# Cross-attention outputs as latents by features, with a column of ones in the values

## Chip, cores and metric

The kernel runs on one core of a Trainium2 chip. The metric is the device time of one execution in microseconds. It is float32 throughout, except where the reference rounds to fp8, which the kernel does by arithmetic on VectorE. In the profile PE is TensorE, PEld its weight loads, DVE VectorE, ACT ScalarE, POOL GpSimd and SP the engine that issues most transfers.

## What is computed

One block of a perceiver: 128 latents of 512 features attend to 12,544 context tokens, then to each other, then pass through a mixture of 32 experts. Nearly all the work is the cross-attention to the context, which, cut to what matters, is

```
k = ctx @ w_k ; v = ctx @ w_v              # 12544 x 1024 each: 8 groups of 128
k = layernorm(k) per group
for g in 8 groups, for the 2 query heads of g:
    p   = softmax(q_h @ k_g.T / sqrt(128))  # 128 latents x 12544 tokens
    out = p @ v_g                           # 128 latents x 128 features
x += fp8_linear(concat(out) / smooth)       # rounded to fp8, then projected to 512
```

## The kernel before

**Chunks.** The tokens go through in 25 chunks `c`, 24 of 512 tokens and one of 256 in the middle (`c = 12`). The softmax is a running one: after each chunk the maxima may grow, and what has been summed so far (`ol[g]`) is scaled down by `exp(old - new)`.

**One chunk.** First the keys of chunk `c` are made (`keys`, `k_chunk`), then for `g` = 0 to 7 `scores(c, g)` alternates with a step of the values (`v_chunk`); the outputs of chunk `c` (`outputs(c, g)`) are spread over the making of the keys of chunk `c + 1`. In `scores`, PE multiplies the keys (tokens stationary) by the queries of two heads, 256 columns, so that a tile `s` has 128 token rows (partitions) and 4 x 256 columns: four token blocks by 2 heads x 128 latents. ACT evicts it from PSUM with the key's norm as a scale (line 919, below called S0 to S7 by group).

**Maxima, shift and exponential.** `maxima` calls `max_rows` for groups in fours; it makes `sh`, the number to subtract, and `als`, the old maxima less the new. `spread(c, j)` then treats groups `2j` and `2j + 1`: DVE spreads `sh` over all partitions by a transposition into PSUM (`b_ps`, line 974), does the same for the scale factors (`al`, in SBUF), and subtracts the shift from both groups' `s` (line 992, one instruction of 128 x 1024 for each group). `weigh` takes the exponential on ACT (line 1004, below E0 to E7 by group), scales `ol[g]` on POOL (line 1006), and adds on POOL the four blocks of `s` into the second half of `ol[g]` (line 1014): sums by lane, which become the softmax's denominators at the very end.

**Outputs.** `outputs` has the values stationary and the 256 columns of `s` moving, four accumulating matmuls for each group; each float32 matmul shows in the profile as two passes, each with its own weight load. The result is 128 features x 256, and DVE adds it to `ol[g]` (line 1027).

**The values.** `v_chunk` makes the values by a Strassen scheme: PSUM banks are accumulated into in several products, and between two products ACT copies the state of a bank out. In

```
            mm(a, 5, False)
            u2 = kept(a, "u2")
            mm(d, 2, False)
            nc.vector.tensor_tensor(t2[:, :H], d, u2, ALU.add)
            mm(a, 6, False)
```

`kept` is an ACT copy of bank `a` (line 439). Product 6 adds to that bank, so PE can't begin it before ACT has made the copy; product 2, into another bank, lies between them. In the profile these are line 562: product 5 is `a_ps<-wsum,mix`, product 2 is `c_ps<-wsum,ctx`, product 6 is the second `a_ps<-wkv,ctx`.

**Order.** Engines work through their own queues in order and wait for each other by semaphores. A scheduler decides at build time, by its own estimate of durations, in which order each queue holds its instructions; `tc.issue_after` only adds a bound. So the program has a fixed order on each engine, which can be read from the built program.

**The end.** After the last chunk `lane_sums` sums the lanes by matmuls with a column of ones, `finished` turns the reciprocals into columns of all partitions and scales, `round_block` rounds to fp8, and `proj` projects, four blocks. Some `spin` matmuls lie between. Then follow self-attention and the experts.

Of the kernel before, what the change touches and what calls it, by code (L numbers as in the profile page):

```python
# [45 lines left out]
def block_kernel(  # L46
# [223 lines left out]
    V = vp.tile([P, CH // P, G * D], F32, name="V")  # L270
# [103 lines left out]

    def v_unit(c, v):

        nt = chunks[c][1] // P

        def mm(ps, i, first):
            w, x = mixed_w[i], mixed[c][i]  # L380
            for k in range(2):
                last_mm[0] = nc.tensor.matmul(
                    ps, lhsT=x[:, k, v * P : (v + 1) * P], rhs=w[:, k, H : 2 * H],
                    start=first and k == 0, stop=k == 1, skip_group_check=True,
                ).ins

        t1, t2 = V[:, v, :], V[:, nt // 2 + v, :]
        return unit(mm, lambda t: t, t1[:, :H], t2[:, :H], t1[:, H:], t2[:, H:])
# [132 lines left out]
    def v_chunk(c):  # L521
# [10 lines left out]
        def both(t):  # L532
            return t.rearrange("p (i o) -> p i o", i=2)

        def to(o, v):
            return V[:, v, :].rearrange("p (i c o) -> p i c o", i=2, c=2)[:, :, o, :]

# [20 lines left out]
        for v in range(2):  # L558
            def mm(ps, i, first):
                w, x = mixed_w[i], mixed[c][i]  # L560
                for k in range(2):
                    last_mm[0] = nc.tensor.matmul(  # L562
                        ps, lhsT=x[:, k, v * P : (v + 1) * P], rhs=w[:, k, H : 2 * H],
                        start=first and k == 0, stop=k == 1, skip_group_check=True,
                    ).ins

            t1, t2 = V[:, v, :], V[:, 2 + v, :]
            a, d = bank("a_ps"), bank("c_ps")
            mm(a, 0, True)
            nc.vector.tensor_tensor(t1[:, :H], a, t1[:, :H], ALU.add)  # L570
            mm(d, 4, True)
            nc.scalar.copy(t2[:, H:], d)
            yield
            mm(a, 5, False)
            u2 = kept(a, "u2")
            mm(d, 2, False)
            nc.vector.tensor_tensor(t2[:, :H], d, u2, ALU.add)
            mm(a, 6, False)
            nc.vector.tensor_tensor(t2[:, H:], a, t2[:, H:], ALU.add)
            added[0] = nc.vector.tensor_tensor(t1[:, H:], a, t1[:, H:], ALU.add).ins  # L580
            yield
# [63 lines left out]
    with tc.tile_pool(name="pre", bufs=2) as pre, tc.tile_pool(name="pre1", bufs=1) as pre1, tc.tile_pool(  # L645
# [248 lines left out]
    ol = [olp.tile([P, 2, HS], F32, name=f"ol{g}") for g in range(G)]  # L894
    rlat = keep.tile([S, NH], F32, name="rlat")
# [3 lines left out]
        tc.tile_pool(name="ps_so", bufs=3, space=PSUM, side="right", reuse_waits="tile")  # L899
    )  # L900
    ps_t = late.enter_context(
        tc.tile_pool(name="ps_t", bufs=2, space=PSUM, side="right", reuse_waits="tile")
    )
    prob, mxr, mrun, shifts, rescale, lsum, summed = {}, {}, {}, {}, {}, {}, [None]
# [28 lines left out]
    def max_rows(c, j0, n):  # L933
# [29 lines left out]
        if c:  # L963
            al = small.tile([P, 32], F32, tag="als", name="als", bufs=3)[:, : 16 * n]
            nc.vector.tensor_tensor(al, old[:, : 16 * n], m, ALU.subtract)  # L965
            nc.scalar.activation(al, al, AF.Exp, scale=scale)  # L966
        for j in range(j0, j0 + n):
            x = slice(16 * (j - j0), 16 * (j - j0) + 16)
            mrun[j] = m[:, 16 * (j - j0) :]
            shifts[j] = sh[:, x], al[:, x] if c else None  # L970

    def to_all(dst, src):

        nc.vector.transpose(  # L974
            dst.rearrange("p h (k i) -> p (h k) i", i=32),
            src[:, :, None].to_broadcast([P, 16, 32]),
        )

    def spread(c, j):

        nt = chunks[c][1] // P
        sh, al = shifts.pop(j)
        ps = ps_t.tile([P, 2, HS], F32, tag="t", name="b_ps")

        with tc.issue_after(added[0]) if whole(c) and j == 2 else nullcontext():
            to_all(ps, sh)
        if c:
            rescale[j] = tmp.tile([P, 2, HS], F32, tag="al", name="al")
            to_all(rescale[j], al)
        for a in range(2):  # L990
            s = prob[2 * j + a]
            nc.vector.tensor_tensor(  # L992
                s[:, :nt, :], s[:, :nt, :], ps[:, a, None, :].to_broadcast([P, nt, HS]),
                ALU.subtract,
            )

    def weigh(c, j, after=None):

        nt = chunks[c][1] // P
        for a in range(2):  # L1000
# [4 lines left out]
            if c:  # L1005
                nc.gpsimd.tensor_tensor(  # L1006
                    ol[g], ol[g], rescale[j][:, a, None, :].to_broadcast([P, 2, HS]), ALU.mult
                )
                first = ol[g][:, 1, :]
            else:  # L1010
                first = s[:, 0, :]

            for t in range(0 if c else 1, 2 if c == NCH - 1 and g >= G - 2 else nt):
                summed[0] = nc.gpsimd.tensor_tensor(ol[g][:, 1, :], first, s[:, t, :], ALU.add).ins  # L1014
                first = ol[g][:, 1, :]

    def outputs(c, g):
        nt = chunks[c][1] // P
        s = prob.pop(g)
        ps = ps_so.tile([D, HS], F32, tag="s", name="o_ps")  # L1020
        for t in range(nt):
            end = nc.tensor.matmul(  # L1022
                ps, lhsT=V[:, t, g * D : (g + 1) * D], rhs=s[:, t, :],
                start=t == 0, stop=t == nt - 1,
            )
        if c:
            nc.vector.tensor_tensor(ol[g][:, 0, :], ol[g][:, 0, :], ps, ALU.add)  # L1027
        else:
            nc.vector.tensor_copy(ol[g][:, 0, :], ps)
        return end.ins  # L1030

    def lane_sums(g, last):

        if g % 4 == 0:
            lsum[g // 4] = ps_t.tile([S, 8], F32, tag="t", name="l_ps")
        ps = lsum[g // 4]
        for h in range(2):
            i = g % 4 * 2 + h
            x = slice(h * S, (h + 1) * S)
            terms = [ol[g][:, 1, x]] + [t[:, x] for t in last]  # L1040
            for t, y in enumerate(terms):
                end = nc.tensor.matmul(
                    ps[:, i : i + 1], lhsT=y, rhs=ones[:, 0:1], start=t == 0,
                    stop=t == len(terms) - 1,
                )
        if g % 2:
            nc.vector.reciprocal(rlat[:, 2 * g - 2 : 2 * g + 2], ps[:, g % 4 * 2 - 2 : g % 4 * 2 + 2])
        return end.ins

    def finished(b):  # L1050


        ps = ps_so.tile([P, 4, S], F32, tag="s", name="ps_inv")
        r0 = _COLS["smooth"][0] + 16 + 4 * b
        for h in range(4):
            end = nc.tensor.transpose(
                ps[:, h, :], rlat[:, 4 * b + h : 4 * b + h + 1].to_broadcast([S, P]), ident
            )
        for h in range(4):
            o = ol[2 * b + h // 2][:, 0, (h % 2) * S : (h % 2 + 1) * S]  # L1060
            nc.vector.scalar_tensor_tensor(
                o, o, rcol[:, r0 + h : r0 + h + 1], ps[:, h, :], ALU.mult, ALU.mult
            )
# [20 lines left out]
    for c in range(NCH):  # L1084
# [7 lines left out]
        for g in range(G):  # L1092
# [10 lines left out]
            if g == 2 and c + 1 < NCH:  # L1103
                with tc.issue_after(summed[0] if c else made):
# [25 lines left out]
    with ExitStack() as rest:  # L1130
# [18 lines left out]
        def round_block(b):  # L1149
            cq = post.tile([P, 4, S], F32, tag="cq", name="cq")  # L1150
            rounded(post, cq, [ol[2 * b + a][:, 0, :].rearrange("p (h s) -> p h s", h=2) for a in range(2)])
            return cq
# [11 lines left out]
        last = {g: prob[g] for g in (G - 2, G - 1)}  # L1164

        def sums_of(g):
            return lane_sums(
                g, [last[g][:, t, :] for t in range(2, CH // P)] if g in last else []
            )

        spare = pps.tile([P, H], F32, tag="ps", name="spare")

# [8 lines left out]

        cqs = {}
        maxima(c, 8)
        outputs(c, 0)
        maxima(c, 9)
        outputs(c, 1)
        outputs(c, 2)
        maxima(c, 10)
        end = outputs(c, 3)
        with tc.issue_after(end):  # L1190
            sums_of(0)
            sums_of(1)
        outputs(c, 4)
        end = outputs(c, 5)
        with tc.issue_after(end):
            finished(0)
            cqs[0] = round_block(0)
            sums_of(2)
            end = sums_of(3)
        with tc.issue_after(end):  # L1200
            outputs(c, 6)
            end = outputs(c, 7)
        with tc.issue_after(end):
            finished(1)
            cqs[1] = round_block(1)
            sums_of(4)
            end = spin(spare[:, :240], sums_of(5), 4)
        with tc.issue_after(end):
            end = proj(0, cqs[0]).ins
        with tc.issue_after(end):  # L1210
            finished(2)
            cqs[2] = round_block(2)
            sums_of(6)
            end = spin(spare[:, :240], sums_of(7), 1)
        with tc.issue_after(end):
            end = finished(3)
            cqs[3] = round_block(3)
        for b in (1, 2, 3):
            with tc.issue_after(end):
                end = proj(b, cqs[b]).ins  # L1220


        mask = post1.tile([P, 4, P], F32, name="mask")
        with tc.issue_after(summed[0]):
# [27 lines left out]
        with tc.tile_pool(name="po_s", bufs=1, space=PSUM, reuse_waits="tile") as pss:  # L1252
# [68 lines left out]
            with tc.issue_after(summed[0]):  # L1321
# [190 lines left out]
```

## Time and profile before

| | |
|---|---|
| median of 3 runs (lowest, highest) | 2119.5 us (2119.05, 2121.09) |
| span of the profiled execution | 2117.6 us |
| PE busy | 2092.5 us, 99% of the span |
| PEld, weight loads, beside PE | 1584.7 us, 75% |
| DVE busy | 1508.2 us, 71% |
| POOL busy | 1180.5 us, 56% |
| ACT busy | 907.8 us, 43% |
| mean granted TensorE clock | 0.997 |

The profile has no other time of the profiled execution than its span, from its first to its last instruction; the median of the runs is 1.9 us more. Matmuls are pipelined and the ends that the profile gives for them are modelled, so how fast they go is best read from the distance between their starts. Busy time of an engine other than PE says how much room it has, not what it costs.

### The profile page before, as it was taken

To read this page: it belongs to the slowest core of one execution; us is meant where nothing else is said; L and a number is where in the kernel's file an instruction comes from. 1 tells how busy PE (TensorE), PEld (TensorE's weight loads), DVE (VectorE), ACT (ScalarE), POOL (GpSimd) and SP (SyncE) were. 2 spreads that over 40 slices of the span, in tenths; PEclk is the share of its full clock that TensorE was granted. 3 is DMA by queue.
4 is the path that set the end of the run, shared out by engine and by line. 5 is a ranking of instruction groups with operands and counts; after the bars stand their busy time and mean duration, and the time that the engine had idled before them with its cause. 6 is when DMAs were issued, how large, how long until landed. Compare 5 with 4: busy or idle time off the path is not lost.

```text
span 2117.6 us, 25404 instructions
## 1 busy us (share of the span) xinstructions
PE 2092.5 (99%) x9087; PEld 1584.7 (75%) x9087; DVE 1508.2 (71%) x2875; ACT 907.8 (43%) x1687; POOL 1180.5 (56%) x1359
## 2 busy tenths in 40 slices
PE   8999999999999999999999999999999999999999
PEld 3667877877887787787777877787787778776554
DVE  8787777678678767866878678767867876786211
ACT  3445455445435544543444445444544544441111
POOL 5345675575576557558675576567557656743000
PEclk9999999999999999999999999999999999999999
DMA  9300000000000000000000000000000000008693
GB/s 324 119 21 1 21 21 0 21 20 21 1 21 21 0 21 20 11 1 21 21 21 20 1 21 20 1 21 20 16 6 21 21 1 21 1 6 303 189 286 108
DMA packets 71231, 95.59 MB, mean 45 GB/s; under 512 B 3136, under 2 KB 39488, under 8 KB 71104
## 3 DMA queue, kind: packets, MB, share of 16 engines
q1 hardware_dynamic: 70816, 93.92, 13.4%
q8 instruction: 71, 1.16, 0.2%
q14 instruction: 56, 0.46, 0.1%
q10 hardware_dynamic: 288, 0.04, 0.0%
HBM read 93.69 MB, written 0.26 MB: 44 GB/s over the span
## 4 chain that ended last, share of the span: by engine, by line
PE 92%; DVE 3%; issue 2%; POOL 1%; ACT 1%; DMA 0%; SPq 0%; POOLq 0%; DVEq 0%; ACTq 0%
PE s_ps L914 15%; PE o_ps L1022 15%; PE a_ps L458 11%; PE a_ps L562 11%; PE c_ps L458 7%; PE c_ps L562 7%; PE gu_ps L1427 4%; PE fa_ps L527 4%; PE fa_ps L449 4%; PE moe_acc L1448 2%; PE fc_ps L449 2%; PE fc_ps L527 2%; PE ps_p L710 2%; PE fb_ps L527 1%; PE fb_ps L449 1%
## 5 line engine op out<-in xcount | busy, mean ns | idle before, releaser
L1014 POOL TENSOR_TENSOR ol<-ol,s 128x256 f32<-128x256 f32 x764 | 549.9, 731 | 46.6 <-ACT s L1004 9.9
L1022 PE MATMUL o_ps<-s,V 128*128 128x256 f32 x1568 | 371.5, 379 | 0.9 <-DVE ol L1027 0.9
L914 PE MATMUL s_ps<-qxT,KT 128*128 128x256 f32 x1568 | 370.2, 379 | 0.4 <-ACT s L919 0.4
L919 ACT ACTIVATE s<-s_ps,krs 128x256 f32<-128x256 f32 x784 | 320.9, 472 | 107.8 <-PE s_ps L914 77.2
L1006 POOL TENSOR_TENSOR ol<-ol,al 128x512 f32<-128x512 f32 x192 | 243.5, 1280 | 209.6 <-DVE al L974 209.6
L914 PEld LDWEIGHTS s_ps<-qxT,KT 128*128 128x128 f32 x1568 | 297.8, 190 | 74.1 <-issue 36.4
L619 POOL TENSOR_TENSOR krs<-kve,mhalf 128x16 f32<-128x16 f32 (+1 forms) x50 | 142.9, 2858 | 358.9 <-DVE kve L617 358.9
L925 DVE TRANSPOSE_TENSOR_REDUCE mxr<-s 128x32 f32<-128x1024 f32 (+1 forms) x200 | 243.9, 1220 | 117.2 <-ACT s L919 115.6
L1022 PEld LDWEIGHTS o_ps<-s,V 128*128 128x128 f32 x1568 | 291.4, 190 | 37.9 <-ACT s L1004 1.3
L1004 ACT ACTIVATE s<-s 128x1024 f32<-128x1024 f32 (+1 forms) x200 | 203.6, 1040 | 85.1 <-DVE s L992 84.7
L992 DVE TENSOR_TENSOR s<-s,b_ps 128x1024 f32<-128x1024 f32 (+1 forms) x200 | 231.5, 1177 | 0.0
L591 ACT ACTIVATE sq<-KT 128x1024 f32<-128x1024 f32 (+1 forms) x100 | 103.8, 1040 | 228.2 <-DVE KT L477 220.8
L1027 DVE TENSOR_TENSOR ol<-ol,o_ps 128x256 f32<-128x256 f32 x192 | 77.7, 405 | 157.3 <-PE o_ps L1022 152.4
L562 PE MATMUL a_ps<-wkv,ctx 128*128 128x512 f32 x368 | 172.9, 592 | 0.0
L458 PE MATMUL a_ps<-ctx,wkv 128*128 128x256 f32 x736 | 170.3, 379 | 0.0
L458 PEld LDWEIGHTS a_ps<-ctx,wkv 128*128 128x128 f32 x736 | 138.1, 190 | 18.1 <-ACT u L439 0.3
L595 DVE TRANSPOSE_TENSOR_REDUCE sqr<-sq 128x32 f32<-128x1024 f32 (+1 forms) x104 | 121.0, 1168 | 4.9 <-ACT sq L591 4.9
L477 DVE TENSOR_TENSOR KT<-a_ps,KT 128x512 f32<-128x512 f32 x138 | 90.0, 681 | 44.1 <-PE a_ps L458 43.4
L562 PEld LDWEIGHTS a_ps<-wkv,ctx 128*128 128x128 f32 x368 | 69.9, 190 | 68.4 <-issue 66.0
L439 ACT COPY u<-fa_ps 128x512 f32<-128x512 f32 x92 | 54.0, 587 | 102.3 <-PE fa_ps L449 100.0
L966 ACT ACTIVATE als<-als 128x32 f32<-128x32 f32 x48 | 11.0, 229 | 198.1 <-DVE als L965 198.1
L1427 PE MATMUL gu_ps<-gu,xT 128*128 128x384 f32 x256 | 87.4, 486 | 0.0
(314 smaller groups left out, 3321.6 us busy)
## 6 DMA issues: line engine op xcount, KB each, us to landing
ctx<-in_ctxT SPq DMA_DIRECT2D x23, 1024.0 KB, 5.0
gu<-in_w SPq DMA_DIRECT2D x32, 384.0 KB, 5.0
gu<-in_v SPq DMA_DIRECT2D x32, 384.0 KB, 5.7
dn<-in_w SPq DMA_DIRECT2D x16, 768.0 KB, 5.5
w<-in_wprojT SPq DMA_DIRECT2D x8, 1024.0 KB, 5.7
w<-in_wqxT SPq DMA_DIRECT2D x4, 1024.0 KB, 11.2
w<-in_wqT SPq DMA_DIRECT2D x4, 1024.0 KB, 5.1
wkv<-in_wkvT SPq DMA_DIRECT2D x8, 256.0 KB, 8.2
```

What stands on the lines that cost most here:

```text
L449: nc.tensor.matmul(ps[:, j * P : (j + 1) * P], lhsT=f[n][:, i, g * D : (g + 1) * D], rhs=xs[i][n], start=first and j == 0, stop=True, skip ...
L458: nc.tensor.matmul(ps[:, j * h : (j + 1) * h], lhsT=w[:, k, (2 * u + j) * D : (2 * u + j + 1) * D], rhs=x[:, k, :], start=first and j == k ...
L562: last_mm[0] = nc.tensor.matmul(ps, lhsT=x[:, k, v * P : (v + 1) * P], rhs=w[:, k, H : 2 * H], start=first and k == 0, stop=k == 1, skip_g ...
L914: end = nc.tensor.matmul(ps[:, t - t0, :], lhsT=KT[:, g, t * P : (t + 1) * P], rhs=qxT[:, 2 * g : 2 * g + 2, :], start=True, stop=True,)
L919: copied[0] = nc.scalar.activation(s[:, t, :], ps[:, t - t0, :], AF.Copy, scale=rs[:, t : t + 1]).ins
L925: nc.vector.tensor_reduce(mxr[g // 4][:, g % 4, :nt, :].rearrange("p t k -> p (t k)"), s[:, :nt, :].rearrange("p t (k i) -> p (t k) i", i=32),
L992: nc.vector.tensor_tensor(s[:, :nt, :], s[:, :nt, :], ps[:, a, None, :].to_broadcast([P, nt, HS]), ALU.subtract,)
L1004: nc.scalar.activation(s[:, :nt, :], s[:, :nt, :], AF.Exp, scale=scale)
L1006: nc.gpsimd.tensor_tensor(ol[g], ol[g], rescale[j][:, a, None, :].to_broadcast([P, 2, HS]), ALU.mult)
L1014: summed[0] = nc.gpsimd.tensor_tensor(ol[g][:, 1, :], first, s[:, t, :], ALU.add).ins
L1022: end = nc.tensor.matmul(ps, lhsT=V[:, t, g * D : (g + 1) * D], rhs=s[:, t, :], start=t == 0, stop=t == nt - 1,)
L1427: nc.tensor.matmul(ps, lhsT=xT[:, k, :], rhs=experts[x][0][i][:, k], start=k == 0, stop=k == NK - 1,)
```

## The change

`outputs` is turned round: the weights `s` are stationary, 128 tokens x 128 latents of one head, and the values move, so the result has latents on partitions and features in columns. A column of ones beside each group's 128 features (V is 129 wide by group) makes the last column of the result the softmax's denominator. The lane sums on POOL are gone, with `lane_sums`, `finished` and the spreading of the scale factors: with latents on partitions the factor is one number per partition, made by four small ACT exponentials. The shift is spread into SBUF in place of PSUM, and of the two subtractions of a `spread` the second (groups 1, 3, 5, 7) is done by POOL. The PSUM banks for scores and outputs go from 3 to 5. At the end each group is divided by its denominator (`averaged`), turned by PE transposes (`turned_block`) and rounded. The diff, cut to its core:

```diff
-    V = vp.tile([P, CH // P, G * D], F32, name="V")
+    V = vp.tile([P, CH // P, G, D + 1], F32, name="V")
+    nc.gpsimd.memset(V[:, :, :, D:], 1.0)
...
-    ol = [olp.tile([P, 2, HS], F32, name=f"ol{g}") for g in range(G)]
+    ol = [olp.tile([S, 2, D + 1], F32, name=f"ol{g}") for g in range(G)]
...
-        tc.tile_pool(name="ps_so", bufs=3, space=PSUM, side="right", reuse_waits="tile")
+        tc.tile_pool(name="ps_so", bufs=5, space=PSUM, side="right", reuse_waits="tile")
...
-            nc.scalar.activation(al, al, AF.Exp, scale=scale)
+            df = df.rearrange("p (x k) -> p x k", k=4)
+            al = small.tile([P, 8], F32, tag="als", name="als", bufs=3)[:, : 4 * n]
+            for b in range(4):
+                x = slice(32 * b, 32 * b + 32)
+                nc.scalar.activation(al[x], df[x, :, b], AF.Exp, scale=scale)
...  spread
-        ps = ps_t.tile([P, 2, HS], F32, tag="t", name="b_ps")
+        b = tmp.tile([P, 2, HS], F32, tag="shift", name="shift")
...
-        if c:
-            rescale[j] = tmp.tile([P, 2, HS], F32, tag="al", name="al")
-            to_all(rescale[j], al)
-        for a in range(2):
+        for a, eng in enumerate((nc.vector, nc.gpsimd)):
             s = prob[2 * j + a]
-            nc.vector.tensor_tensor(
-                s[:, :nt, :], s[:, :nt, :], ps[:, a, None, :].to_broadcast([P, nt, HS]),
+            scaled[0] = eng.tensor_tensor(
+                s[:, :nt, :], s[:, :nt, :], b[:, a, None, :].to_broadcast([P, nt, HS]),
                 ALU.subtract,
-            )
+            ).ins
...  weigh
-                nc.gpsimd.tensor_tensor(
-                    ol[g], ol[g], rescale[j][:, a, None, :].to_broadcast([P, 2, HS]), ALU.mult
-                )
-                first = ol[g][:, 1, :]
...
-            for t in range(0 if c else 1, 2 if c == NCH - 1 and g >= G - 2 else nt):
-                summed[0] = nc.gpsimd.tensor_tensor(ol[g][:, 1, :], first, s[:, t, :], ALU.add).ins
-                first = ol[g][:, 1, :]
+                scaled[0] = nc.gpsimd.tensor_tensor(
+                    ol[g], ol[g], al[:, 2 * a : 2 * a + 2, None].to_broadcast([S, 2, D + 1]),
+                    ALU.mult,
+                ).ins
...  outputs
-        ps = ps_so.tile([D, HS], F32, tag="s", name="o_ps")
-        for t in range(nt):
-            end = nc.tensor.matmul(
-                ps, lhsT=V[:, t, g * D : (g + 1) * D], rhs=s[:, t, :],
-                start=t == 0, stop=t == nt - 1,
-            )
+        ps = ps_so.tile([S, 2, D + 1], F32, tag="s", name="o_ps")
+        for h in range(2):
+            for t in range(nt):
+                end = nc.tensor.matmul(
+                    ps[:, h, :], lhsT=s[:, t, h * S : (h + 1) * S], rhs=V[:, t, g, :],
+                    start=h == t == 0, stop=t == nt - 1, skip_group_check=True,
+                )
...  at the end, in place of lane_sums and finished
+        def averaged(g):
+            rl = small.tile([S, 2], F32, tag="rl", name="rl")
+            nc.vector.reciprocal(rl, ol[g][:, :, D])
+            for h in range(2):
+                nc.vector.tensor_scalar(
+                    ol[g][:, h, :D], ol[g][:, h, :D], rl[:, h : h + 1], None, ALU.mult
+                )
+        def turned_block(b):
+            ps = ps_so.tile([P, 4, S], F32, tag="s", name="h_ps")
+            for h in range(4):
+                end = nc.tensor.transpose(ps[:, h, :], ol[2 * b + h // 2][:, h % 2, :D], ident)
+            cq = post.tile([P, 4, S], F32, tag="cq", name="cq")
+            quantise(post, cq, ps, "smooth", 16 + 4 * b)
+            return end.ins, cq
```

The changed program is known as it was built, with the order of every queue. On PE that order is the same as before in the chunks, but for the sixteen passes of a group's outputs in place of eight. On ACT it differs in one stretch of every whole chunk but the first, 23 of 25:

```
before:  S5   u2<-a_ps   E0 E1 E2   S6   E3 ...
after:   S5   E3   u2<-a_ps   E0 E1 E2   S6 ...
```

and POOL's queue there holds: subtraction of group 1, scaling of `ol0` and `ol1`, subtraction of group 3, scaling of `ol2` to `ol7`, subtractions of groups 5 and 7. DVE's holds the transposition of the shift for groups 0 and 1, that for groups 2 and 3, and then the subtractions of groups 0 and 2.

## The prediction

> **What bounds the kernel now.** I read the page's first part, then the chain, then one steady chunk by stretches.
>
> ```profile
> PE 2092.5 (99%) x9087; PEld 1584.7 (75%) x9087; DVE 1508.2 (71%) x2875; ACT 907.8 (43%) x1687; POOL 1180.5 (56%) x1359
> PE 92%; DVE 3%; issue 2%; POOL 1%; ACT 1%; DMA 0%; SPq 0%; POOLq 0%; DVEq 0%; ACTq 0%
> 1308.34:1382.69 74.35, 74.35 (x333) 58.69 (x332) 55.70 (x101) 34.57 (x62) 46.88 (x55) 1.00 0.05 15
> ```
>
> The last line is one chunk by stretch (length; busy time of PE, PEld, DVE, ACT, POOL; clock). PE works 74.35 of 74.35 us. So what is taken from POOL or DVE is worth nothing there, what is added to PE counts in full, and a new wait of PE counts in full. The change is to be judged by two things: what the turned outputs cost PE, and whether some queue now makes PE wait.
>
> **The columns.** PE's timeline (start, length, passes) has both shapes side by side:
>
> ```profile
> 1085.27 0.61 PE L449 MATMUL fb_ps<-ctx,wkv 128*128 128x128 f32 x4
> 1085.71 0.61 PE L449 MATMUL fb_ps<-mix,wkv 128*128 128x128 f32 x4
> 1086.16 0.61 PE L449 MATMUL fa_ps<-ctx,wkv 128*128 128x128 f32 x4
> 1086.61 0.61 PE L449 MATMUL fa_ps<-mix,wkv 128*128 128x128 f32 x4
> 1087.05 1.89 PE L1022 MATMUL o_ps<-s,V 128*128 128x256 f32 x8
> 1088.78 1.05 PE L449 MATMUL fc_ps<-finer,finer 128*128 128x128 f32 x8
> ```
>
> Sixteen passes of 128 columns take 1087.05 - 1085.27 = 1.78 us, 111.5 ns each; eight of 256 take 1088.78 - 1087.05 = 1.73, 216 ns each. There are 1568 passes of outputs before, 3136 of 129 columns after. Each 256 turns into two at 111.5: 223 - 216 = 7 ns, times 1568 = 11 us slower. Bounds: by proportion to the wide pass (129/256 of 216 = 108.8) 2.5 us; by the slowest distance above (0.45/4 = 112.5) 14 us. I take 11, the row one column away.
>
> **What leaves or comes beside PE.** POOL loses 764 lane additions of 731 ns (559 us), 192 scalings shrink from 1280 to some 735 ns, and 100 subtractions come. DVE loses half its subtractions and the spreading of the factors (96 of 0.67 us). ACT gets six more small exponentials a chunk, 6 x 0.23 = 1.4 us where it has 40 idle. Together nothing: PE covers it. Two more banks: PE waits for none in this chunk, nothing.
>
> **The wait that comes.** This is the part that decides. In the steady chunk ACT's u2 copy lies between products 5 and 6 of the values. Timelines of PE, ACT and DVE:
>
> ```profile
> 1291.15 1.88 PE L562 MATMUL a_ps<-wsum,mix 128*128 128x512 f32 x4
> 1292.87 1.88 PE L562 MATMUL c_ps<-wsum,ctx 128*128 128x512 f32 x4
> 1294.58 1.88 PE L562 MATMUL a_ps<-wkv,ctx 128*128 128x512 f32 x4
> ...
> 1293.12 0.59 ACT L439 COPY u<-a_ps 128x512 f32<-128x512 f32 x1
> 1293.60 2.01 ACT L1004 ACTIVATE s<-s 128x1024 f32<-128x1024 f32 x2
> 1300.80 1.07 ACT L1004 ACTIVATE s<-s 128x1024 f32<-128x1024 f32 x1
> ...
> 1290.80 0.73 DVE L974 STREAM_TRANSPOSE b_ps<-sh 128x512 f32<-128x512 f32 x1
> ```
>
> The copy ends at 1293.71, product 6 starts at 1294.58: cover 0.87 us. E3 comes at 1300.80, long after. In the changed program's ACT queue E3 stands before that copy, in 23 chunks, and E3 reads group 3's `s`, which POOL now subtracts. So the copy, and PE's product 6 behind it, wait for POOL. Behind E3 on ACT are the copy, E0 to E2 and the evictions of S6.
>
> When is POOL done? The shift for groups 0 and 1 is written at 1290.80 + 0.73 = 1291.53; POOL has finished the finer tokens by then (in the next chunk at 1361.4, 4 us ahead). POOL's rows give 731 ns for 256 columns and 1280 for 512, so 2.145 ns a column: 2.38 us for a subtraction of 1024. Its queue is subtraction, two scalings of 0.735, subtraction: 2 x 2.38 + 2 x 0.735 = 6.23, end at 1297.76. E3 takes 1.06 and the copy 0.59: 1299.4. Product 6 was due at 1294.58: PE stands for 4.8 us.
>
> That is without a quarrel between DVE and POOL. Before, DVE's subtraction read the shift from PSUM; now both its operands are in SBUF. The trace has one such instruction under way while POOL works:
>
> ```profile
> 35.30 1.26 POOL L728 TENSOR_TENSOR qb_t<-pnn,kb 128x512 f32<-128x512 f32 x1
> 35.37 1.74 DVE L238 TENSOR_TENSOR x_v_in<-qz_z,qz_m 128x512 f32<-128x512 f32 x1
> 44.66 0.67 DVE L238 TENSOR_TENSOR x_q_in<-qz_z,qz_m 128x512 f32<-128x512 f32 x1
> ```
>
> The same line takes 0.67 us alone and 1.74 beside POOL: it ends at 37.11, 0.55 us after POOL's 36.56. They take turns. The two DVE subtractions (1.2 us each) are issued from 1292.2 on, inside POOL's four instructions, so all six go one after the other: 6.23 + 2.4 = 8.63, end at 1300.16; E3 and copy to 1301.8; PE stands 7.2 us. I take 7.2, as the rows have the same operation on operands in the same places. Lowest: no turns, and POOL at the pace of its fastest row of 512 (L692, 1041 ns: 1.90 and 0.62), 3.6 us.
>
> **The clock.** A stall of that length costs more than itself.
>
> ```profile
> 1962.43:1972.67 10.24, 9.82 (x36) 7.56 (x36) 1.69 (x5) 1.74 (x4) 0.00 (x0) 0.50 0.27 93
> 8.68 3.75 PE L382 MATMUL a_ps<-wkv,ctx 128*128 128x512 f32 x4 [1.63 <-DMA ctx<-in_ctxT]
> 12.22 2.05 PE L382 MATMUL b_ps<-wkv,ctx 128*128 128x512 f32 x3
> ```
>
> The granted clock falls to 0.50 for 10.24 us after a thin stretch of self-attention, and again 2.3 us after the last matmul; an idle 1.95 us at 998.8 didn't lower it. 7.2, and also 4.8, are beyond. At the program's start dense passes of 512 run 0.89 us apart in place of 0.43 from 8.68 until 13.42, where the clock record begins at 1.00: 4.74 us at half speed, 2.4 lost. I take 2.4 for each stall, the row of the same event (dense work after idleness); bounds 0 and half of 10.24, 5.1.
>
> [...]
>
> **The other half of the chunk.** E5 and E7 wait for POOL too, and the u3 copy stands behind E5. By the same count, with turns, POOL ends group 5 at 1317.1, E5 ends at 1318.2, the copy at 1318.9; PE wants it at 1319.7. Cover 0.8 us, cost nothing; if it is gone, 1 us of delay costs 23 us. The outputs themselves have 11 us and more.
>
> **The end.** PE sheds 48 passes of lane sums at 0.111 (5.3 us), ten spins at 0.203 (2.0) and a wait of 0.9; the 16 transposes of reciprocals are replaced by 16 of heads. Against that, group 4's outputs wait for E5 and E4, both behind POOL, and DVE's queue gets 24 small instructions between the roundings. Following it I get the last projection at about 1941, as before. I take 0, bounds -8.2 and +6. Chunks 0 and 12 have an exponential of POOL's group ahead of evictions: 2 us for both, 0 to 8.
>
> **The sum.** 2117.6 + 11 + 23 x (7.2 + 2.4) + 2 = 2351 span; the median of the runs lies 1.9 above the span: 2352.
>
> **Rivals.**
> A, above, 0.63.
> B, DVE and POOL don't take turns at this size: stall 4.8, 23 x 7.2 = 166, total 2298. For: DVE's 32-column additions show no delay beside POOL. Against: the row shown. 0.14.
> C, the stall comes but the clock stays: 23 x 7.2 = 166, total 2298 as well; or with neither turns nor clock 23 x 4.8 = 110, 2243. Against: the clock's fall after 2.3 us. 0.07.
> D, the delay spreads (cover of u3 gone too, banks late): 2 us more in each chunk, 2398, or beyond. 0.07.
> E, E3's place doesn't matter, as POOL is far quicker: only columns and end, 2132. For it POOL would have to finish group 3 by 1292.9, 1.4 us after the shift; a single subtraction takes more. 0.05.
> F, faster. One place: the end of the last chunk. Price: the 8.2 us that PE sheds there, all of it kept, against 2.5 for columns at proportion: 2114. It decides only where E3 holds nothing up and a pass takes under 110.6 ns (2 x 110.6 - 216 = 5.2 ns, x1568 = 8.2). The 16-pass row speaks against the second, POOL's durations against the first. 0.04, of which 0.02 fall within 0.2%.
>
> **Numbers.** A is the likeliest: 2352. The range has as its low end the lowest stall without clock (23 x 3.6 = 83, total 2214) and as its high end turns with the largest clock loss (23 x 12.3 = 283, total 2414); it leaves out E, F and part of D, 0.13 or so. Some 0.2% (4 us) is what can be told from no change here: faster 0.02, same 0.02, slower 0.96.
>
> **What would show it.** Right: in each whole chunk PE idle by some 7 us before the second `a_ps<-wkv,ctx`, put down to ACT's u2 copy, and that to the exponential waiting for POOL's subtraction; PEclk below 9; 129-column passes 111 to 112 ns apart; DVE's subtraction of group 0 well over 1.2 us. Wrong: PE still full in mid-kernel (then E), POOL and DVE subtractions at 2.4 and 1.2 us side by side (B), clock at 1.00 throughout (C).

## The result, and the profile after

The changed kernel takes 2338.7 us (median of 4 runs, 2336.4 to 2341.1), the kernel before on the same chip 2120.3: a ratio of 1.1028, 95% interval 1.1013 to 1.1044. The forecast was 2352 in a range of 2214 to 2414. The profiled execution has a span of 2336.6 us, 219.0 more than before.

From the page: busy time by engine, the chain that ended last, and the group of product 6 (busy, mean ns of one, idle time before it and what ended it).

```profile
PE 2158.0 (92%) x10597; PEld 1656.2 (71%) x10597; DVE 1458.2 (62%) x2683; ACT 949.6 (41%) x1831; POOL 824.6 (35%) x688
...
PE 74%; DVE 10%; POOL 9%; ACT 4%; issue 3%; DMA 0%; POOLq 0%; SPq 0%; DVEq 0%; ACTq 0%
...
L570 PE MATMUL a_ps<-wkv,ctx 128*128 128x512 f32 x368 | 214.2, 713 | 146.4 <-ACT u L447 146.4
```

POOL and DVE are less busy than before, as the change set out to make them, and both are now on the chain (9% and 10%, where they had 1% and 3%). PE stands, and in one place. The waits of PE and of ACT (total, times, longest) say who holds whom:

```profile
PE a_ps L570 <- ACT u L447: 146.4, 23, 6.4
ACT s L1006 <- POOL s L993: 174.3, 72, 5.5
```

23 waits of 6.4 us, one in each of the 23 whole chunks in which E3 stands ahead of the u2 copy. One of them in the timeline (start, length):

```profile
1428.22 2.36 POOL L993 TENSOR_TENSOR s<-s,shift 128x1024 f32<-128x1024 f32 x1 [4.73 <-DVE shift L987]
...
1428.59 4.62 DVE L993 TENSOR_TENSOR s<-s,shift 128x1024 f32<-128x1024 f32 x2
...
1429.35 1.88 PE L570 MATMUL c_ps<-wsum,ctx 128*128 128x512 f32 x4
...
1430.53 3.16 POOL L1008 TENSOR_TENSOR ol<-ol,als 128x258 f32<-128x258 f32 x2
...
1433.65 2.34 POOL L993 TENSOR_TENSOR s<-s,shift 128x1024 f32<-128x1024 f32 x1
...
1436.02 1.06 ACT L1006 ACTIVATE s<-s 128x1024 f32<-128x1024 f32 x1 [5.51 <-POOL s L993]
1436.98 0.57 ACT L447 COPY u<-a_ps 128x512 f32<-128x512 f32 x1
...
1437.60 3.58 PE L570 MATMUL a_ps<-wkv,ctx 128*128 128x512 f32 x4 [6.37 <-ACT u L447]
```

Read it from the bottom. Product 6 waits for the u2 copy; the copy stands in ACT's queue behind E3; E3 waits until POOL's second subtraction ends at 1435.99. Above that, POOL's two scalings take 3.16 us and DVE's two subtractions 4.62: the six instructions take turns from 1428.22 to 1435.99, each ending after the one before it (POOL at 1430.58, DVE 1431.66, POOL 1432.13, DVE 1433.21, POOL 1433.69 and 1435.99). And product 6 itself, four passes, shows 3.58 us where it showed 1.88 before.

The same chunk by stretches, the stall and what follows (length; busy time of PE, PEld, DVE, ACT, POOL; clock):

```profile
1431.23:1437.60 6.37, 0.00 (x1) 0.00 (x0) 3.16 (x4) 1.58 (x3) 5.91 (x5) 0.72 0.00 1
1437.60:1444.50 6.90, 6.90 (x17) 3.81 (x18) 2.64 (x4) 4.47 (x7) 0.00 (x0) 0.76 0.00 0
```

The clock falls during the stall (0.50 from 1434.03 to 1440.86) and is still down when PE resumes. Measured by the distance between the starts of passes, against the usual distance for their shape, product 6 begins 6.53 us late and the passes of the next 12 us lose another 1.69 or 2.81 us, in turns from chunk to chunk.

### The profile page after: what moved, and what is told of

Read it like the earlier page. It is cut to its first block, busy times and chain, and to the rows that moved or that the text cites. A ratio compares the mean times of both kernels' runs of the same rounds, so it can differ in the third digit from the quotient of the medians.

```text
span 2336.6 us, 27690 instructions
## 1 busy us (share of the span) xinstructions
PE 2158.0 (92%) x10597; PEld 1656.2 (71%) x10597; DVE 1458.2 (62%) x2683; ACT 949.6 (41%) x1831; POOL 824.6 (35%) x688
## 4 chain that ended last, share of the span: by engine, by line
PE 74%; DVE 10%; POOL 9%; ACT 4%; issue 3%; DMA 0%; POOLq 0%; SPq 0%; DVEq 0%; ACTq 0%
PE o_ps L1019 14%; PE s_ps L918 10%; PE a_ps L466 10%; PE a_ps L570 8%; PE c_ps L466 7%; POOL s L993 5%; PE gu_ps L1383 4%; POOL ol L1008 3%; PE c_ps L570 3%; PE fa_ps L457 3%; DVE mxr L929 3%; PE fa_ps L535 3%; PE moe_acc L1404 2%; ACT s L923 2%; DVE m_new L956 2%
## 5 line engine op out<-in xcount | busy, mean ns | idle before, releaser
L1019 PE MATMUL o_ps<-V,s 128*128 128x129 f32 x3136 | 384.8, 276 | 2.3 <-ACT s L1006 2.3
L1019 PEld LDWEIGHTS o_ps<-V,s 128*128 128x128 f32 x3136 | 377.3, 193 | 9.7 <-ACT s L1006 2.7
L918 PE MATMUL s_ps<-qxT,KT 128*128 128x256 f32 x1568 | 380.6, 387 | 0.0
L570 PE MATMUL a_ps<-wkv,ctx 128*128 128x512 f32 x368 | 214.2, 713 | 146.4 <-ACT u L447 146.4
L993 POOL TENSOR_TENSOR s<-s,shift 128x1024 f32<-128x1024 f32 (+1 forms) x100 | 276.3, 2773 | 136.1 <-DVE shift L987 136.1
L1008 POOL TENSOR_TENSOR ol<-ol,als 128x258 f32<-128x258 f32 x192 | 161.4, 866 | 449.4 <-ACT als L974 449.4
L993 DVE TENSOR_TENSOR s<-s,shift 128x1024 f32<-128x1024 f32 (+1 forms) x100 | 221.9, 2237 | 0.0
L1024 DVE TENSOR_TENSOR ol<-ol,o_ps 128x258 f32<-128x258 f32 x192 | 78.8, 410 | 181.8 <-PE o_ps L1019 178.5
L974 ACT ACTIVATE als<-dfs 32x8 f32<-32x8 f32 x192 | 41.0, 213 | 200.9 <-DVE dfs L969 198.9
L466 PE MATMUL c_ps<-mix,wsum 128*128 128x256 f32 x368 | 87.1, 380 | 0.4 <-ACT KT L505 0.4
```

The costliest lines, as they stand in the source:

```text
L466: nc.tensor.matmul(ps[:, j * h : (j + 1) * h], lhsT=w[:, k, (2 * u + j) * D : (2 * u + j + 1) * D], rhs=x[:, k, :], start=first and j == k ...
L570: last_mm[0] = nc.tensor.matmul(ps, lhsT=x[:, k, v * P : (v + 1) * P], rhs=w[:, k, H : 2 * H], start=first and k == 0, stop=k == 1, skip_g ...
L918: end = nc.tensor.matmul(ps[:, t - t0, :], lhsT=KT[:, g, t * P : (t + 1) * P], rhs=qxT[:, 2 * g : 2 * g + 2, :], start=True, stop=True,)
L993: scaled[0] = eng.tensor_tensor(s[:, :nt, :], s[:, :nt, :], b[:, a, None, :].to_broadcast([P, nt, HS]), ALU.subtract,).ins
L1008: scaled[0] = nc.gpsimd.tensor_tensor(ol[g], ol[g], al[:, 2 * a : 2 * a + 2, None].to_broadcast([S, 2, D + 1]), ALU.mult,).ins
L1019: end = nc.tensor.matmul(ps[:, h, :], lhsT=s[:, t, h * S : (h + 1) * S], rhs=V[:, t, g, :], start=h == t == 0, stop=t == nt - 1, skip_grou ...
```

## Experiments

The theory: E3's place ahead of the u2 copy makes the stall; its length comes of POOL's queue with DVE and POOL taking turns; the fall of the clock adds to it; the turned outputs by themselves cost little. The rivals: POOL too slow wherever E3 stands; no turns; a clock that costs nothing; turned outputs as the loss.

**E3 behind the copy.**

```diff
-            wait = (c, j) in ((0, 3), (NCH // 2 - 1, 2)) or whole(c) and j != 1
+            wait = (c, j) in ((0, 3), (NCH // 2 - 1, 2)) or whole(c)
```

> All exponentials of a whole chunk, those of groups 2 and 3 too, are issued only after ACT's last copy, so ACT's queue is u2 copy, E0, E1, evictions of S6, E2, E3; POOL still does half of the subtractions and nothing else is changed. Theory (the place of E3 ahead of the u2 copy is the cause): product 6 waits for nothing, PE is full again, the clock stays at 1.00; 2117.6 + 12.5 for the columns + some 5 for chunks 0 and 12 and the tail = 2135, at most 2145. Rival (POOL is simply too slow for its half, wherever E3 stands): some other wait of PE takes its place, 2230 or more. Rival (turned outputs cost by themselves): close to 2338.

Measured: 2138.2 us, ratio 1.0091 (1.0073 to 1.0110). One condition takes back 200 of the 218 us, with POOL's half and the turned outputs still there. A steady chunk by stretches:

```profile
1438.04:1512.95 74.91, 74.91 (x398) 60.75 (x397) 53.44 (x93) 36.34 (x69) 32.03 (x26) 1.00 0.05 15
```

PE is full and the clock is 1.00. The group of DVE's subtractions still has a mean of 2237 ns in this run: the slow subtractions are there, and cost nothing in the steady chunk as nobody waits for them. In the whole chunks POOL's slowness is a price only through E3's place.

**The place alone, in the kernel before.**

```diff
-            u2 = kept(a, "u2")
+            with tc.issue_after(expd[0]) if v == 0 else nullcontext():
+                u2 = kept(a, "u2")
...
-                nc.scalar.activation(s[:, :nt, :], s[:, :nt, :], AF.Exp, scale=scale)
+                expd[0] = nc.scalar.activation(s[:, :nt, :], s[:, :nt, :], AF.Exp, scale=scale).ins
...
+            if whole(c) and g == 5:
+                maxima(c, 5)
+                maxima(c, 6)
...
-            maxima(c, g)
+            if not (whole(c) and g in (5, 6)):
+                maxima(c, g)
```

> The kernel before, with nothing of the change but the place of E3: spreads, subtractions and exponentials of groups 0 to 3 are issued one step earlier, and ACT's u2 copy of the first half of the values only after E3; the scores of group 6 and the second half's first product are kept behind product 6, as they are in both kernels. All subtractions are DVE's with the shift in PSUM, the lane sums stay on POOL, the outputs have 256 columns. Theory (the place of E3 does it, whoever makes its operand): DVE needs 2 x (0.73 + 0.67 + 2.4) = 7.6 us from 1290.8 to the last subtraction, then 1.06 + 0.59: PE stands some 5 us (4 to 6) and loses 2.2 more to the clock, 23 x 7.2 = 166, total 2285 (2260 to 2305). Rival (it takes POOL's slowness to make the stall): 2120 to 2150.

Measured: 2295.3 us, ratio 1.0823 (1.0808 to 1.0837). The first line of PE's waits:

```profile
PE a_ps L563 <- ACT u L440: 134.7, 23, 5.9
```

5.9 us in 23 chunks without a single subtraction on POOL. ACT's queue here is E0 to E3, then the copy; E3 comes last, and its operand is DVE's fourth subtraction, so DVE alone gets it ready late enough. Some 7.6 us a chunk, where 7.2 were expected. So the order on ACT's queue is enough to make the stall, whichever engine is late.

**The turns.**

```diff
-        b = tmp.tile([P, 2, HS], F32, tag="shift", name="shift")
+        halves = [
+            ps_t.tile([P, 2, HS], F32, tag="t", name="b_ps")[:, 0, :],
+            tmp.tile([P, HS], F32, tag="shift", name="shift"),
+        ]
...
+        for a in (1, 0):
...
+                nc.vector.transpose(
+                    halves[a].rearrange("p (k i) -> p k i", i=32),
+                    sh[:, 8 * a : 8 * a + 8, None].to_broadcast([P, 8, 32]),
+                )
```

> E3 stays ahead of the u2 copy, but DVE reads its half of the shift from PSUM and only POOL's half lies in SBUF (two transposes of half the width, POOL's first; two of the five banks for outputs and scores are given to it). Theory (DVE and POOL take turns when both of a DVE operation's operands lie in SBUF): DVE's subtractions go back to 1.2 us and POOL's queue ends at 2 x 2.36 + 2 x 0.615 = 5.95 after its start in place of 7.77, and starts some 0.3 earlier; PE's idle falls from 6.37 to about 4.3 in each of 23 chunks, total 2338.7 - 23 x 2.1 = 2290. Rival (no turns; POOL's queue alone sets it and DVE is slow for another reason): idle 6.0 or more, total 2330 or more.

Measured: 2291.5 us, ratio 1.0816 (1.0797 to 1.0835). The stall's start in the timeline, with E3 still ahead of the copy:

```profile
1400.75 2.36 POOL L999 TENSOR_TENSOR s<-s,shift 128x1024 f32<-128x1024 f32 x1 [4.46 <-ACT als L977]
...
1401.18 1.18 DVE L999 TENSOR_TENSOR s<-s,b_ps 128x1024 f32<-128x1024 f32 x1
...
1403.08 1.19 POOL L1014 TENSOR_TENSOR ol<-ol,als 128x258 f32<-128x258 f32 x2
...
1404.23 2.34 POOL L999 TENSOR_TENSOR s<-s,shift 128x1024 f32<-128x1024 f32 x1
```

DVE's subtraction takes 1.18 us inside POOL's 2.36, and neither waits; POOL's two scalings go from 3.16 to 1.19. POOL's queue ends 5.82 us after its start in place of 7.77, PE's idle is 4.15 us (95.5 in 23 waits) in place of 6.37. The turns are real and were worth 2.2 us a chunk: 4.62 us for two of DVE's subtractions beside POOL with both operands in SBUF, 1.18 for one with its shift in PSUM. What makes the engines take turns, no run shows.

**The clock.**

```diff
+FILL = 6
...
+            for _ in range(FILL if v == 0 else 0):
+                with tc.issue_after(after):
+                    after = nc.tensor.matmul(
+                        filled, lhsT=ident, rhs=qxT[:, 0:4, :], start=True, stop=True
+                    ).ins
             mm(a, 6, False)
```

> After, with six matmuls of 512 columns on PE (12 passes, 5.15 us at full clock) between product 2 and product 6 of the first half of the values, written to a bank that nobody reads; E3 stays where it is, so product 6 waits as long as before. Theory (the idle time itself lowers the clock): idle left of some 1.2 us, clock 1.00 throughout, and the 2.2 us a stall that the half clock costs are gone: 2338.7 - 51 = 2288. Rival (the clock's fall costs nothing, or comes of something else than idling): 2335 to 2340, or above if the fill delays something.

Measured: 2285.3 us, ratio 1.0787 (1.0771 to 1.0803). PE does 5.15 us of useless work in each chunk and the kernel is 53 us faster for it. The wait for the copy is down to 28.2 us in 23 times, and a whole chunk has a clock of 1.00. It takes 81.48 us by the starts of scores, where the whole chunks of the changed kernel take 83.07 and 84.19 in turns: the half clock's price is 2.15 us a stall, some 49 in all. The other 4 us lie behind the last chunk, where the clock is at half for 13.65 us in the changed kernel and for 6.83 in this run.

How it depends on the idle time, with 0 to 5 filling matmuls by chunk:

> The run with the fill, but with 0 to 5 matmuls of 512 columns, by the chunk's number modulo 6; each takes 0.86 us, so PE's idle before product 6 is 6.4, 5.5, 4.6, 3.8, 2.9 and 2.1 us. To be read is what each chunk loses at half clock. Theory (a fall of the clock is one event, with a least idle time and a fixed price): about 2.2 us for each idle of 3.8 and more, nothing at 2.1 or so; 2.9 is open. Rival (price in proportion to the idle time): 2.2, 1.9, 1.6, 1.3, 1.0, 0.7. [...]

Measured in one execution (2326.9 us), by the start distances of the 12 us after product 6 (0.1 of each loss is there at full clock too). Idle 2.1 us: 0.1 us in each of four chunks, no fall. Idle 2.9: 0.1 in two chunks, 1.7 in two. Idle 3.8: 1.7, 2.8, 2.9, 1.7. Idle 4.6: 2.7, 1.7, 1.8, 2.9. Idle 5.5 to 6.4: 1.5 to 3.1. Two chunks with the same idle, from the timeline:

```profile
474.90 1.55 PE L571 MATMUL a_ps<-wkv,ctx 128*128 128x512 f32 x3 [2.93 <-ACT u L448]
...
972.09 2.93 PE L571 MATMUL a_ps<-wkv,ctx 128*128 128x512 f32 x3 [2.94 <-ACT u L448]
```

Three passes take 1.55 us after one stall and 2.93 after another of equal length. So it is an event that happens or doesn't, with a price of 1.5 to 3.1 us, about the same at 3.8 as at 6.4 us of idle time: the rival, a price in proportion, is out. The records of half clock in this run last 3.41, 6.83 or 10.24 us. Idle times of 2.9 us lowered the clock in two chunks of four, so 2.9 isn't yet safe; of the doses, 2.1 us is the longest that lowered it in no chunk.

**The turned outputs alone.** First with both subtractions on DVE and the shift still in SBUF:

```diff
-        for a, eng in enumerate((nc.vector, nc.gpsimd)):
+        for a, eng in enumerate((nc.vector, nc.vector)):
```

> Both subtractions of each pair on DVE again, the outputs still latents by features with the column of ones; the shift stays in SBUF. The order on ACT becomes u2 copy, E0 to E3, as in the kernel before. Theory: no stall, DVE has room (some 12 us more of 74 a chunk than after), 2117.6 + 12.5 + 3 = 2133: this is the price of the turned outputs alone. Rival (the outputs turned are the loss): 2250 or more. Rival (columns at proportion): 2120.

Measured: 2164.1 us, ratio 1.0215 (1.0200 to 1.0231). A miss by 31, and far from both rivals. No E3 stall and no POOL subtraction, and yet PE waits for DVE in two places, 12.7 us for `KT` and 7.4 for `V`. POOL's scalings and its mixing of the next chunk's tokens also read SBUF, and DVE's four subtractions take turns with them. Three of them, and two mixing steps, which take 1.28 us in the kernel before:

```profile
1419.28 6.41 DVE L993 TENSOR_TENSOR s<-s,shift 128x1024 f32<-128x1024 f32 x3
...
1422.35 2.26 POOL L304 TENSOR_TENSOR ctx<-ctx 128x512 f32<-128x512 f32 x1
...
1424.57 2.25 POOL L305 TENSOR_TENSOR mix<-ctx,mix 128x512 f32<-128x512 f32 x1
```

Then the same with the shift in PSUM:

```diff
-        b = tmp.tile([P, 2, HS], F32, tag="shift", name="shift")
+        b = ps_t.tile([P, 2, HS], F32, tag="t", name="b_ps")
...
-        for a, eng in enumerate((nc.vector, nc.gpsimd)):
+        for a, eng in enumerate((nc.vector, nc.vector)):
```

> The turned outputs and the column of ones alone: the shift is written to PSUM as before and both subtractions are DVE's (two banks for it, three for scores and outputs, as before). It is the run with DVE only, with the shift out of SBUF. Theory (that run's 26 us above the run with all waits are DVE's subtractions taking turns with POOL's token mixing, 1.2 to 2.3 us apiece): subtractions back at 1.2 us, no wait of fc_ps in the chunks, 2117.6 + 12.5 for the columns + 5 = 2135. Rival (four subtractions on DVE are too many there, wherever the shift lies): 2155 to 2165. Rival (turned outputs are free once nothing waits): 2120.

Measured: 2126.6 us, ratio 1.0028 (1.0017 to 1.0038), 8 below the theory and 7 above the last rival. DVE's subtractions in the two kernels, shift in SBUF and in PSUM, from their pages:

```profile
L993 DVE TENSOR_TENSOR s<-s,shift 128x1024 f32<-128x1024 f32 (+1 forms) x200 | 317.5, 1616 | 0.1
```

```profile
L996 DVE TENSOR_TENSOR s<-s,b_ps 128x1024 f32<-128x1024 f32 (+1 forms) x200 | 230.2, 1180 | 0.0
```

87 us of DVE's time and 37 of the kernel's lay in where the shift is kept. (The banks for scores and outputs go from five to three with it; PE waits for none of them in the whole chunks of either run.) The turned outputs by themselves cost 6 us.

**The column of ones.**

```diff
-                    ps[:, h, :], lhsT=s[:, t, h * S : (h + 1) * S], rhs=V[:, t, g, :],
+                    ps[:, h, :D], lhsT=s[:, t, h * S : (h + 1) * S], rhs=V[:, t, g, :D],
```

> The turned-only run without the column of ones in the products: passes of 128 columns, and the denominators are left out (a constant 1 takes their place). To be read is the length of a steady chunk: 74.36 us with 64 passes of 256, 74.91 with 128 passes of 129. Theory (a pass of 128 columns already lies at the pace of its weight load, so the 129th column is free, and all of the 0.55 us comes of splitting one pass into two): 74.9. Rival (the passes go by their columns, and the column of ones is the loss): 128 x 0.87 ns less, 74.80.

Measured in one execution (2128.8 us). The first scores of two chunks in a row, with 129 columns and with 128:

```profile
1426.62 1.68 PE L921 MATMUL s_ps<-qxT,KT 128*128 128x256 f32 x7
...
1501.53 1.68 PE L921 MATMUL s_ps<-qxT,KT 128*128 128x256 f32 x7
```

```profile
1426.60 1.68 PE L923 MATMUL s_ps<-qxT,KT 128*128 128x256 f32 x7
...
1501.50 1.68 PE L923 MATMUL s_ps<-qxT,KT 128*128 128x256 f32 x7
```

74.91 and 74.90 us: the column is free. Why it is, by the weight load as the theory has it or otherwise, this run doesn't show. The 0.55 us over the chunk of before are left to the turned form itself: two passes in place of one of 256 columns, with the operands exchanged.

**Both troubles out, POOL's half kept.** The condition of the first experiment and the halves of the third together.

> The change with both of its troubles taken out, and POOL's half kept: E3 behind the u2 copy (all exponentials wait for ACT's last copy) and DVE's half of the shift in PSUM, POOL's in SBUF. Theory (the stall and the turns are all that POOL's half costs in the steady chunks, and the turned-only run at 2126.6 is the floor of this form): a steady chunk of 74.91 us, as in the turned-only run, chunks 0 and 12 some 3 us dearer for their exponentials behind POOL, 2130 in all (2125 to 2135). Rival (POOL's half costs by itself, 15 us as in the run with all waits, where the shift lay in SBUF): 2138. Rival (freeing DVE of 1.2 us x 96 brings something): below 2122.

Measured: 2140.1 us, ratio 1.0093 (1.0076 to 1.0110). A miss by 10: no stall and no turns, and still 13 us behind the turned outputs alone. By the starts of scores, a steady chunk takes 75.37 us in place of 74.91, some 10 us in all. By the distance between the starts of passes all of the 0.46 us lies in one place, in 21 chunks: PE begins the keys' `a_ps` late, as it waits for DVE's addition into `KT`, which empties a bank. DVE and PE there:

```profile
1479.83 0.40 DVE L993 STREAM_TRANSPOSE shift<-sh 128x256 f32<-128x256 f32 x1
1480.16 1.18 DVE L999 TENSOR_TENSOR s<-s,b_ps 128x1024 f32<-128x1024 f32 x1
1481.26 0.68 DVE L485 TENSOR_TENSOR KT<-fb_ps,p 128x512 f32<-128x512 f32 x1
...
1481.99 1.99 PE L466 MATMUL a_ps<-ctx,wkv 128*128 128x256 f32 x8 [0.19 <-DVE KT L485]
```

DVE at the same place in the run of the turned outputs alone:

```profile
1466.59 1.31 DVE L990 STREAM_TRANSPOSE b_ps<-sh 128x512 f32<-128x512 f32 x2
1467.80 0.67 DVE L485 TENSOR_TENSOR KT<-fb_ps,p 128x512 f32<-128x512 f32 x1
1468.39 1.20 DVE L996 TENSOR_TENSOR s<-s,b_ps 128x1024 f32<-128x1024 f32 x1
```

With the shift in halves the addition stands behind a third transposition and a subtraction; otherwise it stands ahead of the subtractions. So the 0.46 us a chunk are again a place in a queue, DVE's this time. They aren't POOL's half as such: the run with all waits has that too, has the addition ahead of the subtractions, and a chunk of 74.91. Nor are they the three banks, which the turned outputs alone have as well. No run has the halves with the addition in its old place. Chunk 0 takes 4.4 us more, where an eviction of scores stands behind an exponential that waits for POOL. The run with all waits loses its 12 us in chunk 0 (8 us), around chunk 12 and at the end. Taking a 1.2 us subtraction off DVE 96 times brought nothing in any run.

No version beat the kernel before. The nearest, the turned outputs alone, is 0.28% behind, and its chunk of 74.91 us is full of PE's work, as the one of before is.

## Why the prediction was right

The mechanism was the one named, E3 ahead of the u2 copy in 23 chunks. The span's 219.0 us against the steps of the sum:

| step | predicted | measured |
|---|---|---|
| stall, 23 times | 7.2 each, 166 | 6.53 each, 150 |
| clock, 23 times | 2.4 each, 55 | 2.15 each, as a mean of two values, 49 |
| columns | 11 | 13.5 |
| chunks 0 and 12, end | 2 | 6 (the rest) |

Two slips of the sum move it by little. Sixteen passes in 1.78 us are 111.25 ns each, not 111.5, and eight in 1.73 us are 216.25, so the rows give 6 ns a pair and 10 us, not 11. The ends of the range are spans, without the 1.9 us that the median lies above the span. And part of the closeness is cancelling: stall and clock came out 22 us smaller than forecast, columns and chunk 0 some 6 larger.

**The stall** was 0.7 us too long. With turns, the six instructions take 7.77 us, not 8.63. POOL's scalings were set at 0.735 us from the row of the lane additions; alone, as in the run with the shift in PSUM, they take 0.6 each. DVE's subtractions add some 2.0 to POOL's queue (7.77 less 5.82), not 2.4. That turns are taken, the step that decided between A and B, was argued from a single instruction early in the trace, and held for all of them; without turns the stall is 4.15 us, where rival B had 4.8, and the kernel takes 2291.5 against B's 2298 (that run pays another 0.46 us a chunk at `KT`, as told above).

**The clock** was 0.25 us a stall too dear, and the 2.15 is a mean of two values: after stalls of the same length 1.69 and 2.81 us are lost in turns (0.1 of each is there at full clock too), by where the record of half clock lies against the stall's end, as told in the last section. Rival C, no loss, is out by the fill.

**The columns** were 2.5 us too cheap. A steady chunk has 64 passes of 256 columns fewer and 128 of 129 more, and goes from 74.36 to 74.91 us: 8.6 ns a pair (0.55 us over 64), not 7, and 13.5 us for 1568 pairs. The starts in the timeline are rounded to 10 ns, too coarse for a difference of 1.6 ns a pass; the length of a whole chunk isn't.

**What was put at nothing.** The u3 copy's cover held: PE has no wait there, rival D is out. Rival E, POOL quick enough, is out by the 23 waits. The banks were worth nothing: a steady chunk takes 74.91 us with five (all waits) and with three (turned outputs alone). The chunks' 13.5 us for columns are not all seen in the turned-only run, which ends 6 us behind: its chunk 12 is 3 us shorter, and its end 1 to 5 us, by how the clock falls there. At full clock, that is with half of the time at half clock taken off, the end would be some 2 us shorter, an estimate from the turned-only run and the run with 128 columns. So of what rival F counted on, the end's shed work, a part is kept, and it doesn't outweigh the columns. In the changed kernel the rest of 6 us is chunk 0's: the second chunk's scores begin at 192.66 us, 6 later than before.

**The idle engines.** The change relieved DVE of 50 us of busy time and POOL of 356, and neither had held PE up. That step of the argument, a gain on an engine that PE covers is worth nothing, is what the runs confirm best: the share kept without stall or turns is no faster than the share given up.

## What to carry to other kernels

Ask of each moved operation not how long it takes but what stands behind its reader in that reader's queue: here a slower subtraction delayed an exponential, behind which an unrelated copy stood that the full engine needed, and a wait condition on one line was worth 200 us. On DVE's queue an addition that came behind a subtraction cost 10. Before work is moved from DVE to POOL, look where the operands lie: here, with both of DVE's in SBUF, the two engines took turns (4.62 us for two of DVE's subtractions, 3.16 for two of POOL's scalings), and with one of DVE's in PSUM they didn't (1.18 for one subtraction, 1.19 for the two scalings). A stall of a busy PE had a second price here, some 2 us in clock (at 2.9 us of idle time in two stalls of four, at 3.8 and more in all), and useless matmuls in the gap bought that back.

## Not expected of the hardware

The price of a fall of the clock is drawn from a few values. In the changed kernel chunks of 83.07 and 84.19 us alternate without exception, with losses of 1.69 and 2.81 us. The record of half clock lasts 6.83 us at each of the 23 stalls, but PE resumes some 3.25 and 5.5 us before the record's end, in turns, and half of that is 1.6 and 2.8. The records start 85.33 and 81.92 us apart in turns (129.71 around chunk 12): 25, 24 and 38 times 3.413 us, which is the shortest record of half clock in this trace. Two chunks make 167.26 us, 49 times 3.413, so that the records lie in the same place in each pair. The end of the kernel shows the same chance: the run with 128 columns and the turned-only run have the same work there, but behind the last scores the clock is at half for 3.41 and 10.24 us in one and for 3.41 in the other, and their spans, 2126.9 and 2122.6, differ by 4.3 us. Differences of 0.2% between kernels of this kind can come of that alone.

DVE and POOL took turns also where the change hadn't put POOL's work: with both subtractions on DVE and the shift in SBUF, they rose from 1.2 to as much as 2.3 us beside POOL's mixing of tokens, and cost the kernel 37 us.
